# Mamba-2 block with LoRA experts in fp32: strided output-weight sums on VectorE, norm sum behind a chunk's products, gate's Silu put off

## The chip, the cores and the metric

The kernel runs on one core of a Trainium2 chip. Its time is the device time of one execution in microseconds (us); the median of several executions counts, and less is better. The core has TensorE (PE in the profile; PEld is its weight load), VectorE (DVE), ScalarE (ACT), GpSimd (POOL) and the queue SP, which issues every DMA of this kernel. Each engine, and SP, carries out its own instructions in the order in which the program holds them, and waits at an instruction whose inputs or buffers are not ready.

## The reference

For x of 2048 positions by 1024 channels, all in fp32:

```python
xn = layernorm(x)
out = x + attn(xn) + ffn(xn)

# attn: a Mamba-2 layer with 64 heads of 64 channels, 8 groups (8 heads each), state size 128
proj = xn @ in_proj_w.T                     # gate (8 x 512), x, B, C (6144), dt (64)
xBC = silu(causal_conv(hbc, kernel 4) + conv_bias)
dt = softplus(dt + dt_bias); dA = exp(-dt * exp(A_log))
state = state * dA[t] + dt[t] * x[t] * B[t]   # over time, per head
y[t] = state . C[t] + x[t] * D
yn = y * rsqrt(mean over the group's 512 channels of y*y + eps) * norm_weight * silu(gate)
attn = yn @ out_proj_w.T

# ffn: a base matrix and LoRA experts (top 2 of 8)
ffn = xn @ W_base.T + b_base + sum over the two experts of w * (xn @ A.T @ B.T) * 2
```

## The kernel before

The work is done in three stages: projections with the scan beside them, then the gates of groups 0 to 5, then the output projection. All large products use a seven-product scheme of Strassen's kind: instead of eight products of quarter matrices it takes seven of their sums, so sums of weights and of operands have to be formed beside TensorE's work.

**The stream of products.** `in_pairs` lists pairs of 128-row weight tiles of the input projection: for each of two sequence halves s and each group g, three pairs that give the raw x, B, C of the group (`raw_d`), and for groups 6 and 7 two pairs that give its gate (`gate_d`, function Silu); at the end come pairs of the base matrix. `pair` works one off in seven products of 8 TensorE instructions each, some 3.6 us a product. Its results leave through `quarter` (made by `stored`): two of four quarters are copied out of PSUM by ScalarE, two are added out of PSUM by VectorE (line 568, tile `ev` of a pool with 4 buffers), where a gate's quarter is then put through Silu by ScalarE in place (line 570). Each is stored by an SP DMA (line 572). Product 4 goes into the PSUM bank that the quarter of product 7 is read from; product 3 lies between them.

**The scan.** A block is (s, g, half): a group over 512 positions. There are 32 blocks, 16 for each s. A block has four slots, c = 0 to 3, one for each chunk of 128 positions; a slot also takes three or four products from the stream. In a slot, the loop issues in this order:

1. one product; at c = 0 `norm_mean` of the previous block (TensorE sums the squares over the channels with a matrix of ones, `ps_nv`; ScalarE takes the root, `rms`, line 866); then `scan_b` of this chunk: on TensorE the products `ps_y` (from the masked product `ms`, which lies in tile `dab`, and from `xdt`), `ps_e` (state with C) and `ps_st` (from `xdd`); on VectorE lines 813, 814 and 828 (ecp, xg, state); on GpSimd the scaling of the state (line 85)
2. `load_decays` of the chunk after next (SP); the first step of `scan_a` of the next chunk (VectorE's scan `es`, line 733)
3. one product; the second step of `scan_a`: `ps_cb` on TensorE, its copies `cbm` and `bt` (lines 744, 746) and x times D (line 751) on ScalarE, the masked product `ms` on VectorE (line 755)
4. two products or one; the third step of `scan_a`: transposes `ps_xt` on TensorE, then 8 activations `xdt` (x times dt, line 766) and 8 activations `xdd` (line 774) on ScalarE

Beside this, slots 1 and 2 hold the convolution of the next block (ScalarE line 683; VectorE line 689, 18 instructions, then Silu on ScalarE, line 677); slot 3 holds `norm_squares` (ScalarE squares, line 854; VectorE sums, lines 857 and 858); slot 0 holds `norm_gate` of the previous block (VectorE's reciprocal, line 872, and products, line 875, then the store of y). `ps_nv` and `ps_cb` share the PSUM bank `aux`.

**Sums of output weights.** In blocks 16 to 31 the loop also forms the sums of the output projection's weights, one of 16 pieces in each block (`out_sums`). A piece is a tile `wo` of 128 x 7 x 4 x 128, and a small tile `wox` of 128 x 7 x 128, one buffer each. It is loaded at the end of slot 0. GpSimd forms four contiguous sums (512 elements in a partition) in slot 1, and four strided ones over the views `t[:, :, k]` (7 runs of 128, 896 elements): two in slot 2 and two in slot 3. Stores stand between these steps. `wox` is written twice for a piece. In block 16 all of this is one slot later and the four strided sums fall into slot 3.

**Order.** The instructions are put in order by a planner, which goes by program order and by its own estimate of when inputs are ready. Some orders are fixed: `mm` and `transpose` keep TensorE in program order, as do `silu`, xdt, xdd and the squares on ScalarE. `gp` keeps GpSimd's sums and state scalings of the second half (s = 1) in program order. `pin` chains VectorE's convolution, scan, scan_b and norm_gate instructions, each behind the one pinned before it. The evictions (line 568), the masked product and the sums of squares are not pinned.

Of the kernel before, what the change touches and what calls it, by code (L numbers as in the profile page):

```python
# [9 lines left out]
AF = mybir.ActivationFunctionType  # L10
ALU = mybir.AluOpType
# [7 lines left out]
HG = H // G  # L19
# [8 lines left out]
P = 128  # L28
TS = 1024
NS = L // TS  # L30
TB = 512
Q = 128
# [11 lines left out]
def mamba_lora_kernel(  # L44
# [17 lines left out]
    nc = tc.nc  # L62
# [17 lines left out]
    def mm(*args, **kw):  # L80
        tc.keep_in_program_order(nc.tensor.matmul(*args, **kw))  # L81
# [6 lines left out]

    pinned = []

    def pin(ins):

        if pinned:
            tc.add_manual_dep(
                ins.ins, pinned[-1].ins.name,
                mybir.DependencyInfo(
                    mybir.DependencyClass.NoSync, mybir.DependencyReason.DATA
                ),
                reason="pin",
            )  # L100
        pinned.append(ins)

    def transpose(out, in_):
        tc.keep_in_program_order(nc.tensor.transpose(out, in_, ident))  # L104
# [455 lines left out]
    def stored(to, first_tile, s, func):  # L560


        def quarter(m, n, ps, add, alu=ALU.add):
            e = ev.tile([P, TB], F32, tag="ev", name="ev")
            if add is None:
                nc.scalar.activation(e, ps, func)
            else:
                nc.vector.tensor_tensor(e, ps, add, alu)
                if func != AF.Copy:
                    nc.scalar.activation(e, e, func)  # L570
            at = s * TS + n * TB
            nc.sync.dma_start(to[:, first_tile + m, at : at + TB], e)

        return quarter

    raw_d = [dram.tile([P, 6, L], F32, tag=f"raw_{g}", name=f"raw_{g}") for g in range(G)]
    gate_d = [dram.tile([P, 4, L], F32, tag=f"gate_{g}", name=f"gate_{g}") for g in range(G)]
# [51 lines left out]
    def products(n, side):  # L629

        nonlocal done
        left = list(side)
        for i in range(n):
            next(stream)
            done += 1
            take = -(-len(left) // (n - i))
            for step in left[:take]:
                step()
            left = left[take:]
        for step in left:  # L640
            step()

    def steps(gen, n):

        return [lambda: next(gen, None) for _ in range(n)]
# [54 lines left out]


    mid_of = {}
    decay_of = {}

    def load_decays(s, g, half, c):
# [18 lines left out]
    def scan_a(s, g, half, c):  # L724

        key = s, g, half, c
        n = f"{s}_{g}_{half}_{c}"
        dab, ecp = decay_of.pop(key)
        hs = slice(g * HG, (g + 1) * HG)
        cs = slice(c * Q, (c + 1) * Q)  # L730

        es = p1.tile([P, HG, Q], F32, tag="es", name=f"es_{n}")
        ins = nc.vector.tensor_tensor_scan(  # L733
            es.rearrange("p h t -> p (h t)"), dab.rearrange("p h t -> p (h t)"), here, 0.0,
            ALU.mult, ALU.add,
        )
# [18 lines left out]
        nc.vector.tensor_tensor(  # L755
            ms, es, cbm.unsqueeze(1).to_broadcast([P, HG, Q]), ALU.mult
        )
        yield
        pst = ps_one.tile([P, 4, Q], F32, tag="st", name=f"ps_xt_{n}")
        for j in range(4):  # L760
            transpose(pst[:, j, :], xg[:, j, cs])
        xdt = p2.tile([P, HG, HP], F32, tag="xdt", name=f"xdt_{n}")
        x_t = pst.rearrange("p j (a q) -> p (j a) q", q=HP)
        for h in range(HG):
            at = g * HG + h
            ins = nc.scalar.activation(  # L766
                xdt[:, h, :], x_t[:, h, :], AF.Copy,
                scale=dt_of[s][:, half * NQ + c, at : at + 1],
            )
            tc.keep_in_program_order(ins)  # L770

        xdd = p1.tile([P, HG, HP], F32, tag="xdd", name=f"xdd_{n}")
        for h in range(HG):
            ins = nc.scalar.activation(  # L774
                xdd[:, h, :], xdt[:, h, :], AF.Copy, scale=es[:, h, Q - 1 : Q]
            )
            tc.keep_in_program_order(ins)
        mid_of[key] = ms, ecp, bt, xdt, xdd, psy
        yield
# [115 lines left out]
    def add(*args):  # L895
        gp(1, *args)
# [39 lines left out]
    def out_sums(pool, i):  # L936

        p, q, kt = i // 8, i // 4 % 2, i % 4
        t = pool.tile([P, 7, 4, P], F32, tag="wo", name=f"wo_{i}")
        x = pool.tile([P, 7, P], F32, tag="wox", name=f"wox_{i}")  # L940

        def store(j, src):
            nc.sync.dma_start(w2_d[p][:, j, :, q, kt, :].rearrange("i c o -> c i o"), src)

        for j, (m, k) in enumerate(((0, 0), (0, 1), (1, 1), (1, 0))):
            nc.sync.dma_start(
                t[:, j].rearrange("c (m k) o -> c m k o", m=2),
                w_out[4 * p + 2 * k : 4 * p + 2 * k + 2, 2 * q + m, :, :, kt, :]
                .rearrange("k c m o -> c m k o"),
            )  # L950
        yield

        add(t[:, 5], t[:, 0], t[:, 3], ALU.subtract)
        add(t[:, 3], t[:, 3], t[:, 2], ALU.add)
        add(t[:, 4], t[:, 3], t[:, 0], ALU.subtract)
        add(t[:, 6], t[:, 1], t[:, 4], ALU.subtract)
        yield
        store(0, t[:, :, 0])
        store(1, t[:, :, 1])
        store(3, t[:, :, 3])  # L960
        yield
        add(x, t[:, :, 0], t[:, :, 2], ALU.subtract)
        add(t[:, :, 2], t[:, :, 2], t[:, :, 3], ALU.add)
        yield
        store(6, x)
        store(4, t[:, :, 2])
        yield
        add(x, t[:, :, 2], t[:, :, 0], ALU.subtract)
        add(t[:, :, 1], t[:, :, 1], x, ALU.subtract)
        yield  # L970
        store(5, x)
        store(2, t[:, :, 1])
        yield


# [67 lines left out]
    for _ in scan_a(*blocks[0], 0):  # L1043
        pass
# [18 lines left out]
    for b, blk in enumerate(blocks):  # L1063
        s, g, half = blk
        prev = blocks[b - 1] if b else None
        nxt = blocks[b + 1] if b + 1 < len(blocks) else None
        for c in range(NQ):
# [8 lines left out]
            n = target(slot) - done  # L1076
# [26 lines left out]
            parts = [side[i * len(side) // np_ : (i + 1) * len(side) // np_] for i in range(np_)]  # L1103
# [10 lines left out]
                    tail = steps(conv_steps, 1)  # L1114

            products(1, parts[0])
            if c == 0 and prev:
                norm_mean(*prev)
            scan_b(*blk, c)
            if 0 < q <= len(quads):  # L1120
                next(quads[q - 1])
            if b == 16 and c == 1:
                left_sums = out_sums(wo, 0)
                next(left_sums)
            elif b >= 16 and c:
                next(left_sums)
                if b == 16 and c == 3:
                    next(left_sums)
                    next(left_sums)
            if second:  # L1130
                load_decays(*second)
            next(a, None)
# [4 lines left out]
            if c == NQ - 1:  # L1137
                sq = norm_squares(*blk)
                parts[1] += steps(sq, 2)
                parts[2] += steps(sq, 1)  # L1140
            products(1, parts[1])
            next(a, None)
            products(1, parts[2])
            products(min(n - 3, 1), parts[3])
            next(a, None)
            for step in tail:
                step()
            for i in range(4, n):
# [404 lines left out]
    for t, (s, p) in enumerate(passes):  # L1553
        last = t + 1 == len(passes)
        for u, i in enumerate(units):
# [10 lines left out]
            if u < 6 or not last:  # L1566
                t1, u1 = (t, u + 1) if u < 6 else (t + 1, 0)
# [153 lines left out]
```

## Time and profile before

| | |
|---|---|
| median of 3 executions | 3442.19 us (3440.59 to 3443.03) |
| the profiled execution | 3442.68 us; its span is 3440.9 us, granted clock 0.995 |
| TensorE busy | 3359.4 us (98% of the span) |
| VectorE busy | 2471.7 us (72%) |
| ScalarE busy | 1524.9 us (44%) |
| GpSimd busy | 959.8 us (28%) |

The busy shares are means over stages that differ. Blocks 0 to 15 are worked off from 179 to 1183 us, blocks 16 to 31 from 1183 to some 2157 us, and the stages of the gates and the output follow. "Idle before" tells how long an engine stood still ahead of an instruction, and the name behind the arrow what ended that wait by the profile; where an instruction waits for more than one engine it is the one that came last. PEclk is the clock that was granted to TensorE, as a share of full speed.

### The profile page before, as it was taken

The page shows a single profiled execution, that of the slowest core. Times are in us where ns is not written, and L with a number is a line of the kernel's source. Part 1 is how long each engine was busy: PE and PEld are TensorE (multiplying, and loading weights), DVE is VectorE, ACT ScalarE, POOL GpSimd, SP SyncE. Part 2 cuts the span into 40 slices and gives each one's busy share as a digit, 9 for nine tenths or more (in the row PEclk, how much of TensorE's full clock was granted, in tenths as well). Part 3 has the DMA queues.
Part 4 walks back from the last instruction along what each step waited for, and adds up shares of the span by engine and source line. Part 5 has one row for each costly group of instructions (what it writes and reads, how often), then busy time and mean ns, then how long its engine had stood idle before and what let it go on. Part 6 is the DMA issues. An engine that isn't in the chain of part 4 may idle for free.

```text
span 3440.9 us, 41344 instructions
## 1 busy us (share of the span) xinstructions
PE 3359.4 (98%) x13828; PEld 2182.9 (63%) x13828; DVE 2471.7 (72%) x2576; ACT 1524.9 (44%) x4030; POOL 959.8 (28%) x611
## 2 busy tenths in 40 slices
PE   9999999999999999999999999999999999999999
PEld 7455555555554445445545445588888888888888
DVE  7379888889887888888888787545644566555654
ACT  2266767676665566666666655222222200000000
POOL 4122222222224333333324333465444100000000
PEclk9999999999999999999999999999999999999999
DMA  6657565666699988888888789676655686585654
GB/s 244 196 162 224 193 212 193 212 199 203 197 312 304 310 248 273 248 260 253 250 270 254 240 261 310 197 237 214 239 184 184 247 318 239 196 299 188 214 164 146
DMA packets 535572, 799.39 MB, mean 232 GB/s; under 512 B 34880, under 2 KB 264384, under 8 KB 531776
## 3 DMA queue, kind: packets, MB, share of 16 engines
q1 hardware_dynamic: 535360, 796.75, 71.4%
q8 instruction: 111, 1.82, 0.2%
q14 instruction: 101, 0.83, 0.1%
HBM read 546.00 MB, written 250.61 MB: 232 GB/s over the span
## 4 chain that ended last, share of the span: by engine, by line
PE 67%; DVE 16%; DMA 6%; ACT 4%; issue 4%; SPq 1%; POOL 1%; DVEq 0%; ACTq 0%; POOLq 0%
PE ps_x_x L81 9%; PE ps_x_w L81 8%; PE ps_y_w L81 5%; PE ps_a_w L81 5%; PE ps_a_x L81 5%; PE ps_y_x L81 5%; PE ps_x_z L81 5%; DVE xg L689 5%; PE ps_a_z L81 3%; PE ps_y_z L81 3%; DVE es L733 2%; PE ps_y L81 2%; PE ps_e L81 2%; PE ps_st L81 2%; PE ps_x_b L81 2%
## 5 line engine op out<-in xcount | busy, mean ns | idle before, releaser
L689 DVE SCALAR_TENSOR_TENSOR xg<-rawx,cw,xg 128x512 f32<-128x512 f32 x384 | 391.1, 1026 | 12.8 <-ACT xg L683 5.4
L85 POOL TENSOR_TENSOR state<-state,tot 128x512 f32<-128x512 f32 x112 | 135.1, 1206 | 812.0 <-PE ps_e L81 775.9
L733 DVE TENSOR_TENSOR_SCAN es<-dab,here 128x1024 f32<-128x1024 f32 x128 | 312.1, 2439 | 12.9 <-ACT xdd L774 7.4
L81 PE MATMUL ps_x_w<-t,w 128*128 128x256 f32 x1344 | 303.8, 379 | 0.0
L751 ACT ACTIVATE ps_y<-xg,dsk 128x128 f32<-128x128 f32 x512 | 189.8, 371 | 239.0 <-DVE xg L814 217.6
L81 PEld LDWEIGHTS ps_x_w<-t,w 128*128 128x128 f32 x1344 | 255.4, 190 | 41.5 <-issue 7.4
L774 ACT ACTIVATE xdd<-xdt,es 128x64 f32<-128x64 f32 x1024 | 262.6, 393 | 0.0
L766 ACT ACTIVATE xdt<-ps_xt,dt 128x64 f32<-128x64 f32 x1024 | 223.8, 337 | 53.7 <-PE ps_xt L104 53.7
L689 DVE SCALAR_TENSOR_TENSOR bc<-rawb,cw,bc 128x512 f32<-128x512 f32 x192 | 192.0, 1003 | 19.4 <-ACT bc L683 15.7
L81 PE MATMUL ps_a_w<-q,w 128*128 128x256 f32 x896 | 202.7, 379 | 2.8 <-DMA w<-w 2.8
L1658 ACT COPY ps_x_w<-ps_a_w 128x512 f32<-128x512 f32 x28 | 16.0, 570 | 418.7 <-PE ps_a_w L81 418.7
L813 DVE TENSOR_TENSOR ecp<-ecp,ps_e 128x512 f32<-128x512 f32 x120 | 81.8, 682 | 160.8 <-PE ps_e L81 156.5
L81 PEld LDWEIGHTS ps_a_w<-q,w 128*128 128x128 f32 x896 | 170.1, 190 | 26.6 <-issue 3.6
L81 PEld LDWEIGHTS ps_y<-dab,xdt 128*64 128x64 f32 x2048 | 112.6, 137 | 110.9 <-ACT xdd L774 81.5
L85 POOL TENSOR_TENSOR wo<-wo 128x512 f32<-128x512 f32 (+1 forms) x80 | 172.3, 2154 | 18.0 <-DMA wo<-in_w_out_dram 13.0
L81 PE MATMUL ps_a_x<-op_again,a_x 128*128 128x512 f32 x384 | 174.4, 597 | 0.0
L81 PE MATMUL ps_y_x<-op_again,s_x 128*128 128x512 f32 x384 | 174.4, 597 | 0.0
L81 PE MATMUL ps_x_x<-op_again,s_x 128*128 128x512 f32 x384 | 172.9, 593 | 1.5 <-ACT ps_x_x L511 1.5
L755 DVE TENSOR_TENSOR dab<-es,cbm 128x1024 f32<-128x1024 f32 x128 | 167.8, 1311 | 7.9 <-ACT cbm L744 7.6
L464 POOL TENSOR_TENSOR s_x<-a_x,a_x 128x512 f32<-128x512 f32 x48 | 73.6, 1534 | 355.1 <-PE ps_y_x L81 200.8
L81 PE MATMUL ps_x_x<-op,s_x 128*128 128x512 f32 x368 | 165.6, 592 | 0.0
L81 PE MATMUL ps_y_x<-op,s_x 128*128 128x512 f32 x368 | 165.5, 592 | 0.0
(320 smaller groups left out, 6884.3 us busy)
## 6 DMA issues: line engine op xcount, KB each, us to landing
w<-w SPq DMA_DIRECT2D x196, 512.0 KB, 3.6
dab<-da_d SPq DMA_DIRECT2D x128, 512.0 KB, 6.3
raw<-ev SPq DMA_DIRECT2D x192, 256.0 KB, 3.8
a_x<-in_w_in_dram SPq DMA_DIRECT2D x168, 256.0 KB, 4.4
w<-wo SPq DMA_DIRECT2D x80, 448.0 KB, 4.4
ecp<-run_d SPq DMA_DIRECT2D x256, 128.0 KB, 5.7
y<-xg SPq DMA_DIRECT2D x64, 512.0 KB, 3.4
rawx<-raw SPq DMA_DIRECT2D x24, 1030.0 KB, 7.3
```

Source lines behind the costliest of these rows:

```text
L81: tc.keep_in_program_order(nc.tensor.matmul(*args, **kw))
L85: ins = nc.gpsimd.tensor_tensor(*args)
L464: nc.gpsimd.tensor_tensor(t[what], t[x], t[y], alu)
L689: ins = nc.vector.scalar_tensor_tensor(dst[:, i, :], raw[:, i, k : k + TB], cw[:, ti, k : k + 1], dst[:, i, :], ALU.mult, ALU.add,)
L733: ins = nc.vector.tensor_tensor_scan(es.rearrange("p h t -> p (h t)"), dab.rearrange("p h t -> p (h t)"), here, 0.0, ALU.mult, ALU.add,)
L751: nc.scalar.activation(psy[:, j, :], xg[:, j, cs], AF.Copy, scale=dsk[:, at : at + 1])
L755: nc.vector.tensor_tensor(ms, es, cbm.unsqueeze(1).to_broadcast([P, HG, Q]), ALU.mult)
L766: ins = nc.scalar.activation(xdt[:, h, :], x_t[:, h, :], AF.Copy, scale=dt_of[s][:, half * NQ + c, at : at + 1],)
L774: ins = nc.scalar.activation(xdd[:, h, :], xdt[:, h, :], AF.Copy, scale=es[:, h, Q - 1 : Q])
L813: pin(nc.vector.tensor_tensor(ecp, ecp, pse, ALU.mult))
L1658: nc.scalar.copy(px, pa)
```

## The change

Three things are moved; the computation stays the same.

- The four strided sums of an output-weight piece go from GpSimd to VectorE, all in slot 3 of the block, in the steps behind the third product. The first is put behind the latest masked product (`behind`), and all four enter the chain of `pin`. The sum that was written into `wox` a second time is now written over `t[:, :, 0]`. The four stores that need them follow at the end of slot 3; the contiguous sums stay on GpSimd in slot 1 (block 16: slot 2), their stores at the end of that slot.
- `norm_mean` is issued behind `scan_b` of slot 0 instead of ahead of it.
- For the two quarters of a gate that VectorE evicts, the Silu and the store are put off: they are kept in a list and issued by `do_put_off`, behind the third step of `scan_a` (xdt and xdd), and behind each product that follows in the slot.

```diff
+    def behind(ins, other):
+        tc.add_manual_dep(ins.ins, other.ins.name, ..., reason="pin")
...
             else:
                 nc.vector.tensor_tensor(e, ps, add, alu)
-                if func != AF.Copy:
+            at = s * TS + n * TB
+
+            def rest():
+                if add is not None and func != AF.Copy:
                     nc.scalar.activation(e, e, func)
-            at = s * TS + n * TB
-            nc.sync.dma_start(to[:, first_tile + m, at : at + TB], e)
+                nc.sync.dma_start(to[:, first_tile + m, at : at + TB], e)
+
+            if add is None or func == AF.Copy:
+                rest()
+            else:
+                put_off.append(rest)
...
+    def do_put_off():
+        while put_off:
+            put_off.pop(0)()
...
-        nc.vector.tensor_tensor(
-            ms, es, cbm.unsqueeze(1).to_broadcast([P, HG, Q]), ALU.mult
-        )
+        masked[:] = [
+            nc.vector.tensor_tensor(
+                ms, es, cbm.unsqueeze(1).to_broadcast([P, HG, Q]), ALU.mult
+            )
+        ]
...
-        add(x, t[:, :, 0], t[:, :, 2], ALU.subtract)
-        add(t[:, :, 2], t[:, :, 2], t[:, :, 3], ALU.add)
+        t0, t1, t2, t3 = (t[:, :, k] for k in range(4))
+        ins = nc.vector.tensor_tensor(x, t0, t2, ALU.subtract)
+        behind(ins, masked[0])
+        pin(ins)
+        pin(nc.vector.tensor_tensor(t2, t2, t3, ALU.add))
+        pin(nc.vector.tensor_tensor(t0, t2, t0, ALU.subtract))
+        pin(nc.vector.tensor_tensor(t1, t1, t0, ALU.subtract))
         yield
         store(6, x)
-        store(4, t[:, :, 2])
-        yield
-        add(x, t[:, :, 2], t[:, :, 0], ALU.subtract)
-        add(t[:, :, 1], t[:, :, 1], x, ALU.subtract)
-        yield
-        store(5, x)
-        store(2, t[:, :, 1])
+        store(4, t2)
+        store(5, t0)
+        store(2, t1)
         yield
...
             products(1, parts[0])
+            scan_b(*blk, c)
             if c == 0 and prev:
                 norm_mean(*prev)
-            scan_b(*blk, c)
...
+            sums_at = (2, 3) if b == 16 else (1, 3)
+            if b >= 16 and c == sums_at[0] or b == 16 and c == 1:
                 next(left_sums)
...
                 parts[1] += steps(sq, 2)
                 parts[2] += steps(sq, 1)
+                if b >= 16:
+                    parts[2] += [lambda: next(left_sums)]
...
             next(a, None)
+            do_put_off()
             for step in tail:
                 step()
             for i in range(4, n):
                 products(1, parts[i])
+                do_put_off()
...
-            if b > 16 or b == 16 and c > 1:
-                if c == 0:
-                    left_sums = out_sums(wo, b - 16)
+            if b > 16 and c == 0:
+                left_sums = out_sums(wo, b - 16)
+                next(left_sums)
+            if b >= 16 and c in sums_at:
                 next(left_sums)
```

More of the change, by code (lines that the diff above doesn't have):

```diff
@@ L89, in mamba_lora_kernel @@
     pinned = []
+    def behind(ins, other):
+        tc.add_manual_dep(
+            ins.ins, other.ins.name,
+            mybir.DependencyInfo(mybir.DependencyClass.NoSync, mybir.DependencyReason.DATA),
+            reason="pin",
+        )
     def pin(ins):
         if pinned:
[L94 to L99, printed above, removed]
-            )
+            behind(ins, pinned[-1])
         pinned.append(ins)
@@ L568, in quarter @@
                 nc.vector.tensor_tensor(e, ps, add, alu)
-                if func != AF.Copy:
+            at = s * TS + n * TB
+            def rest():
+                if add is not None and func != AF.Copy:
                     nc.scalar.activation(e, e, func)
-            at = s * TS + n * TB
-            nc.sync.dma_start(to[:, first_tile + m, at : at + TB], e)
-        return quarter
+                nc.sync.dma_start(to[:, first_tile + m, at : at + TB], e)
[3 more added lines that the diff above has]
+                put_off.append(rest)
+        return quarter
+    put_off = []
+    def do_put_off():
+        while put_off:
+            put_off.pop(0)()
     raw_d = [dram.tile([P, 6, L], F32, tag=f"raw_{g}", name=f"raw_{g}") for g in range(G)]
@@ L702, in mamba_lora_kernel @@
     mid_of = {}
+    masked = []
     decay_of = {}
@@ L754, in scan_a @@
         ms = dab
-        nc.vector.tensor_tensor(
-            ms, es, cbm.unsqueeze(1).to_broadcast([P, HG, Q]), ALU.mult
-        )
+        masked[:] = [
+            nc.vector.tensor_tensor(
+                ms, es, cbm.unsqueeze(1).to_broadcast([P, HG, Q]), ALU.mult
+            )
+        ]
         yield
@@ L1123, in mamba_lora_kernel @@
                 left_sums = out_sums(wo, 0)
+            sums_at = (2, 3) if b == 16 else (1, 3)
+            if b >= 16 and c == sums_at[0] or b == 16 and c == 1:
                 next(left_sums)
[L1125 to L1129, printed above, removed]
             if second:
```

## The prediction

> **What bounds the kernel now.** I read the page first, then the busy time by stage, then who TensorE waits for in the stage that the change works on, then the timeline around the longest of these waits.
>
> ```profile
> PE 3359.4 (98%) x13828; PEld 2182.9 (63%) x13828; DVE 2471.7 (72%) x2576; ACT 1524.9 (44%) x4030; POOL 959.8 (28%) x611
> ```
>
> TensorE has work for 3359.4 of 3440.9 us, so only its 81.5 us of idle time, and time at a lower clock, can be won. By stage (start and end, length, then PE busy, PEld, DVE, ACT, POOL, granted clock, DMA):
>
> ```profile
> 179.00:1183.00 1004.00, 980.33 (x3873) 514.09 (x3872) 858.57 (x1008) 660.22 (x1858) 278.69 (x186) 0.99 0.69 225
> 1183.00:2157.00 974.00, 938.80 (x3697) 485.19 (x3697) 815.74 (x756) 602.80 (x1750) 359.25 (x188) 0.99 0.86 261
> ...
> 1248.00:1253.00 5.00, 4.88 (x27) 3.38 (x28) 0.06 (x1) 1.67 (x2) 0.02 (x1) 0.66 0.41 131
> 1907.00:1915.00 8.00, 6.11 (x10) 2.86 (x11) 3.87 (x5) 7.71 (x22) 0.00 (x0) 0.57 1.04 344
> ```
>
> 1183 to 2157 us is blocks 16 to 31, where the output weights are summed: TensorE idles 974.0 - 938.8 = 35.2 us there. The last two rows show a second cost: behind a long stall the clock is granted at 0.66 over 5 us (5 x 0.34 = 1.7 us lost) or 0.57 over 8 us (3.4 lost). Stretches at 1224, 1777 and 2115 us also read 0.66, so the clock costs 4 x 1.7 + 3.4 = 10.2 us more. The stage can give 45 us at most. Who ends TensorE's waits in it (total, times, longest):
>
> ```profile
> PE ps_xt L104 <- ACT xg L677: 7.5, 4, 3.5
> PE ps_y L81 <- ACT xdt L766: 6.7, 2, 4.4
> PE ps_nv L81 <- DVE sq L858: 3.7, 1, 3.7
> PE ps_nv L81 <- ACT xdt L766: 3.3, 3, 1.1
> ...
> PE ps_nv L81 <- ACT xdd L774: 2.5, 2, 1.7
> PE ps_y L81 <- issue: 2.5, 1, 2.5
> ```
>
> Behind these, on the other engines:
>
> ```profile
> POOL wox L85 <- DMA w<-wox: 55.1, 9, 16.6
> ...
> ACT ev L570 <- DVE ev L568: 20.2, 5, 6.6
> ```
>
> The timeline shows how they become stalls:
>
> ```profile
> 1770.78 3.09 DVE L755 TENSOR_TENSOR dab<-es,cbm 128x1024 f32<-128x1024 f32 x1
> ...
> 1775.96 0.63 ACT L570 ACTIVATE ev<-ev 128x512 f32<-128x512 f32 x1 [6.58 <-DVE ev L568]
> ...
> 1776.85 2.13 PE L81 MATMUL ps_y<-dab,xdt 128*64 128x128 f32 x16 [4.37 <-ACT xdt L766]
> ...
> 2102.19 2.08 POOL L85 TENSOR_TENSOR wox<-wo 128x896 f32<-128x896 f32 x1 [16.63 <-DMA w<-wox]
> ```
>
> At 1775.96 ScalarE stood 6.58 us at a gate's Silu, waiting for the eviction on VectorE; x times dt was queued behind it and TensorE stalled 4.37 us. VectorE was late because GpSimd's strided sums ran: the masked product took 3.09 us (1.22 alone, at 1547.27). At 2102.19 the second strided sum waited for the store of wox's earlier contents; the state's scaling stood behind it in GpSimd's queue, VectorE waited 5.59 us for that at 2107.46, and TensorE 2.48 at 2114.77.
>
> **The sums.** The change takes 64 instructions (4 in each of 16 blocks) off GpSimd and puts them on VectorE.
>
> ```profile
> L689 DVE SCALAR_TENSOR_TENSOR xg<-rawx,cw,xg 128x512 f32<-128x512 f32 x180 | 192.4, 1075 | 4.1 <-ACT xg L683 0.2
> L85 POOL TENSOR_TENSOR wox<-wo 128x896 f32<-128x896 f32 x32 | 75.3, 2354 | 56.5 <-DMA w<-wox 55.1 <-DMA ecp<-run_d 1.4
> ...
> L1464 DVE TENSOR_TENSOR t<-q 128x1024 f32<-128x1024 f32 x28 | 34.1, 1219 | 3.6 <-DMA q<-yg 3.6
> ```
>
> Price on VectorE: 512 elements from SBUF take 686 ns (acc from acc and e, in the last stage, where GpSimd is idle), 1024 take 1219, so 896 take 686 + 533 x 384/512 = 1086 ns; 64 are 69.5 us, 4.34 a block. No row shows VectorE on the strided view; bounds are 0.69 us (no row of 512 is shorter) and 2.7 us (GpSimd's 75.3 + 55.2 + 42.0 us for its 64). I take 1.09: on GpSimd the stride costs nothing (2.07 us for 896 at best, 1.27 for 512, both about 2.4 ns an element). What goes: a conv step (L689) takes 0.75 us alone and 1075 ns (xg, 180) or 1165 ns (bc, 90) on average here, an excess of 58.5 + 37.4 = 96 us; the scan, the masked product and the rest add about 35. The strided sums are 172.5 of the 289.7 us of GpSimd's weight sums, so some 60% of 131 us, 78 us, leaves VectorE. Its total thus hardly changes; the load moves from the third slot, which it fills, to the end of the fourth, behind the masked product and, by program order, behind the norm's squares. There is room:
>
> ```profile
> 1548.40 0.68 DVE L858 TENSOR_TENSOR sq<-sq 128x512 f32<-128x512 f32 x1
> 1552.48 0.69 DVE L813 TENSOR_TENSOR ecp<-ecp,ps_e 128x512 f32<-128x512 f32 x1 [3.40 <-PE ps_e L81]
> ...
> 1549.24 1.10 PE L81 MATMUL ps_nv<-sq,ones 128*128 128x512 f32 x2 [1.11 <-ACT xdt L766]
> ```
>
> VectorE idles 3.40 us there (2.3 to 5.7 in the other blocks). The sums overrun it by about 1 us, and L813, L814, L828 and the next scan wait behind them. The cover for that is the next masked product: it ended at 1561.08 and was first needed at 1564.31, 3.2 us later. So 0, and with the cover gone 1 us a block. The four stores now stand together in SP's queue behind the last sum, ahead of later loads; those have about a slot in hand, 0 again. An eviction caught behind the sums can cost 4.34 + 0.68 - 3.6 (one product of cover) = 1.4 us; as two evictions in 34 us of products meet a 4.3 us stretch only in a few blocks, 4 us in all.
>
> Stalls that this ends: 2.48 us at 2114.77 with 1.7 of clock; 3.74 at 1248.12 with 1.7 (strided sums had stretched conv, squares and mask in block 16); 3.47 at 1908.89 with 3.4 (ps_xt behind a late conv, in part a Silu). Together 16.5 us. Smaller waits behind conv (the rest of ps_xt on xg, ps_x_x and ps_x_g on ev, ps_x_x on a ScalarE copy, ps_y and ps_st on xdd) are 10 us; I count half, 5. Not ended: 2.76 us and its 1.7 at 1224.55, where the sums left on GpSimd run.
>
> **The Silu.** ScalarE's work is the same; its place is behind the 16 activations of xdt and xdd, and its store moves with it past SP's later entries; the gate is read blocks later. The tile ev is held some 5 us longer, of 4 buffers at 4 evictions in some 25 us or more: 0. Gain: 4.37 us at 1776.85 with 1.7, and 2.30 at 1946.68: 8.4 us. What is late next is the conv chain itself.
>
> **The norm's sum.** ps_nv starts 0.16 us behind the end of L858 (1549.08), so its real releaser is that sum, though the view names xdt. The chunk's products need the masked product, which ended 0.6 us sooner. Over the blocks with such a wait this gives 0.6 us each in 21, 24, 29 and 30, 1.2 in 19 and 1.2 in the whole first stage: 4.8 us. It moves 3.0 us later (ps_y, ps_e, ps_st), which also covers L858. Against it: xdd, which the wait had covered, is now met by ps_st, 0.2 us in a dozen blocks, 3 us at most.
>
> **Sum.** 16.5 + 5 + 8.4 + 4.8 = 34.7 us, less 4 + 3 = 7: a gain of 27.7. The profiled execution took 3442.7 us, 1.8 beyond its span and 0.5 above the median of 3442.2; that gives 3415.
>
> The Trainium skill (TensorE: Matmul & The Clock Gate, Why this matters for your kernels) warns only of idle gaps above about 3 us; here the clock fell behind 2.48 and 2.76 us too. By that rule 2115's 1.7 us would not count and the sum would be 3416; the trace disagrees. The Trainium skill (SBUF — State Buffer, Who interferes with whom) lets a VectorE instruction with two SBUF inputs and a reading GpSimd instruction block each other, whichever came second. It speaks against the new sums where they meet the state's scaling. By that rule, at 1.04 us (the scaling's row at 2106.38) in 15 blocks, VectorE would lose up to 16 us, most of it inside the 3.2 us cover; the long conv rows agree with it.
>
> **Rivals.** *Sums at GpSimd's price.* At 2.07 us each a block's sums are 8.3 us; less 3.4 idle and 3.2 cover, 1.7 us stall TensorE in each of 15 block ends, 26 us, and half of them lose 1.7 of clock, 13: 39 against 27.7 of gain, 3453. It decides above about 1.9 us a sum. Against it: the straight line through VectorE's own rows. *The norm's bank.* ps_cb reuses ps_nv's bank aux and comes one product (3.4 us) behind it; the root took from 0.3 to 5.4 us to start after ps_nv, mostly 1.2 to 2.8, and lasts 0.69. Were it late by 1.5 us in all 31 blocks, 46 us would be lost: 3461. *Half of it.* The slots stay late, since conv still runs beside the contiguous sums, and the fourth slot only swaps contention for sums: 8.4 + 4.2 + 4.8 - 7 = 10 us, 3432. *No difference.* Instructions fall into another order and as many stalls form elsewhere: 3442.
>
> **Numbers.** Forecast 0.62, half of it 0.17, no difference 0.07, sums dear 0.09, bank 0.05. About 0.2% (7 us) is what a measurement can tell. The first two give faster 0.79; the last two slower 0.14. The range starts at 3400, the stage's 45 us nearly all won, and ends at 3441, which takes in the half gain and no difference and leaves out the slower cases.
>
> **What would show it.** Right: strided rows on VectorE near 1.09 us; L689 in blocks 16 to 31 below 950 ns; no GpSimd wait for wox; no wait of L570 ahead of xdt; TensorE's idle time in the second stage near 17 us instead of 35, and one 0.66 stretch left in it. Wrong: L813 waiting behind sums and ps_y for the masked product in the second slot, ps_cb waiting for the root, or ps_x_x for evictions behind sums.

## The result, and the profile after

The changed kernel takes **3408.34 us** (median of 4, 3407.0 to 3414.4) against 3442.61 us beside it: a ratio of **0.9905 [0.9888, 0.9922]**, 34.3 us less. The forecast was 3415, a gain of 27.7. The page's line of busy times:

```profile
PE 3351.6 (98%) x13828; PEld 2181.4 (64%) x13828; DVE 2474.4 (73%) x2640; ACT 1522.1 (45%) x4030; POOL 779.9 (23%) x547
```

VectorE has 64 instructions more and yet only 2.7 us more busy time; GpSimd loses 179.9 us. By stage (blocks 0 to 15, then 16 to 31, then five microseconds out of the second; columns as before: start and end, length, busy time of PE, PEld, DVE, ACT, POOL, granted clock, DMA share, GB/s):

```profile
178.00:1187.00 1009.00, 982.79 (x3871) 516.18 (x3870) 856.86 (x1007) 657.00 (x1854) 273.75 (x186) 0.99 0.69 224
1187.00:2123.00 936.00, 927.07 (x3698) 480.08 (x3697) 819.50 (x823) 603.57 (x1755) 185.79 (x124) 1.00 0.91 272
1229.00:1234.00 5.00, 4.78 (x11) 2.24 (x12) 4.96 (x6) 4.66 (x19) 0.00 (x0) 0.66 0.70 227
```

The second stage is 38 us shorter (974.0 to 936.0), the first 5 us longer (1004 to 1009), and TensorE idles 8.9 us in the second where it idled 35.2. The last row is the one stretch at a lower clock left in it, in block 16, where the forecast left one. Who ends TensorE's waits in this stage now (total, times, longest):

```profile
PE ps_y L81 <- ACT xdd L792: 3.4, 2, 2.5
PE ps_xt L105 <- DVE state L846: 2.0, 1, 2.0
PE ps_x_b L81 <- DVE ev L569: 1.7, 1, 1.7
```

Of the three costly lines of before, ps_xt behind conv and ps_nv behind the squares are gone, and ps_y behind xdt is down from 6.7 us to 0.4. The groups of the same stage, one shape a line (busy time, mean ns of one, idle time before):

```profile
L704 DVE SCALAR_TENSOR_TENSOR xg<-rawx,cw,xg 128x512 f32<-128x512 f32 x180 | 149.1, 834 | 5.8 <-ACT xg L698 1.8
L704 DVE SCALAR_TENSOR_TENSOR bc<-rawb,cw,bc 128x512 f32<-128x512 f32 x90 | 103.8, 1161 | 3.6 <-ACT bc L698 2.0
L831 DVE TENSOR_TENSOR ecp<-ecp,ps_e 128x512 f32<-128x512 f32 x64 | 43.6, 682 | 54.5 <-PE ps_e L81 50.0 <-DMA w<-wo 3.2 <-DMA s_x<-s_x_d 1.3
L986 DVE TENSOR_TENSOR wo<-wo 128x896 f32<-128x896 f32 x16 | 20.4, 1272 | 0.5
L985 DVE TENSOR_TENSOR wo<-wo 128x896 f32<-128x896 f32 x16 | 19.0, 1188 | 0.4
L984 DVE TENSOR_TENSOR wo<-wo 128x896 f32<-128x896 f32 x16 | 17.4, 1090 | 0.5
L981 DVE TENSOR_TENSOR wox<-wo 128x896 f32<-128x896 f32 x16 | 17.3, 1084 | 0.0
```

The last four lines are the strided sums, 74.1 us together. Each finds its predecessor just ended (idle 0.0 to 0.5 us over 16). The conv steps of xg (L704, L689 before) fell from 1075 to 834 ns; those of bc, beside the contiguous sums that stay on GpSimd, stayed at 1161. Two lines of the kernel before, in the same stage, go with this: bc's steps, and VectorE's wait for ps_e ahead of ecp.

```profile
L689 DVE SCALAR_TENSOR_TENSOR bc<-rawb,cw,bc 128x512 f32<-128x512 f32 x90 | 104.6, 1165 | 4.4 <-ACT bc L683 2.6
```

```profile
DVE ecp L813 <- PE ps_e L81: 102.3, 34, 6.6
```

The means hide two kinds of steps. Before, 115 of the 180 steps of xg ran beside no GpSimd instruction and took 748 ns on average (753 at most); the 30 that overlapped a strided sum alone took 2235 ns. In the changed kernel 148 run alone, at 747 ns.

VectorE's wait for ps_e ahead of ecp (L831) is 50.0 us here and was 102.3 us: the sums took the idle time that the prediction pointed to, 52 us in 16 blocks, 3.3 us each.

A second profile of the same kernel (below) has TensorE idle for 25.0 us in the first stage and 12.4 in the second, with the stages 1003.2 and 929.4 us long where the first profile has 1009.0 and 923.8 (blocks 0 to 15, and block 16 to the beginning of the last slot). The split between the stages thus moves by some 6 us from one execution to the next while the total moves by 0.6; a single profile tells no more of a stage than that.

### The profile page after: what moved, and what is told of

It is laid out like the page before. It is cut to its first block, busy times and chain, and to the rows that moved or that the text cites. A ratio compares the mean times of both kernels' runs of the same rounds, so it can differ in the third digit from the quotient of the medians.

```text
span 3407.6 us, 41304 instructions
## 1 busy us (share of the span) xinstructions
PE 3351.6 (98%) x13828; PEld 2181.4 (64%) x13828; DVE 2474.4 (73%) x2640; ACT 1522.1 (45%) x4030; POOL 779.9 (23%) x547
## 4 chain that ended last, share of the span: by engine, by line
PE 77%; DVE 12%; ACT 4%; DMA 3%; issue 3%; SPq 0%; POOL 0%; DVEq 0%; ACTq 0%; POOLq 0%
PE ps_x_x L81 11%; PE ps_x_w L81 9%; PE ps_a_x L81 7%; PE ps_y_x L81 7%; PE ps_a_w L81 6%; PE ps_y_w L81 6%; PE ps_x_z L81 5%; DVE xg L704 3%; PE ps_y_z L81 3%; PE ps_a_z L81 3%; PE ps_e L81 3%; PE ps_y L81 3%; PE ps_st L81 2%; PE ps_x_b L81 2%; DVE es L749 2%
## 5 line engine op out<-in xcount | busy, mean ns | idle before, releaser
L704 DVE SCALAR_TENSOR_TENSOR xg<-rawx,cw,xg 128x512 f32<-128x512 f32 x384 | 342.2, 899 | 16.8 <-ACT xg L698 5.9
L749 DVE TENSOR_TENSOR_SCAN es<-dab,here 128x1024 f32<-128x1024 f32 x128 | 297.8, 2326 | 14.5 <-DMA dab<-da_d 10.2
L704 DVE SCALAR_TENSOR_TENSOR bc<-rawb,cw,bc 128x512 f32<-128x512 f32 x192 | 191.0, 1001 | 18.4 <-ACT bc L698 15.0
L772 DVE TENSOR_TENSOR dab<-es,cbm 128x1024 f32<-128x1024 f32 x128 | 164.8, 1287 | 10.3 <-ACT cbm L760 10.0
L81 PE MATMUL ps_a_x<-op,a_x 128*128 128x512 f32 x368 | 165.5, 592 | 0.0
L831 DVE TENSOR_TENSOR ecp<-ecp,ps_e 128x512 f32<-128x512 f32 x120 | 81.8, 682 | 103.9 <-PE ps_e L81 97.8
```

The costliest lines, as they stand in the source:

```text
L704: ins = nc.vector.scalar_tensor_tensor(dst[:, i, :], raw[:, i, k : k + TB], cw[:, ti, k : k + 1], dst[:, i, :], ALU.mult, ALU.add,)
L749: ins = nc.vector.tensor_tensor_scan(es.rearrange("p h t -> p (h t)"), dab.rearrange("p h t -> p (h t)"), here, 0.0, ALU.mult, ALU.add,)
L772: nc.vector.tensor_tensor(ms, es, cbm.unsqueeze(1).to_broadcast([P, HG, Q]), ALU.mult)
L831: pin(nc.vector.tensor_tensor(ecp, ecp, pse, ALU.mult))
```

## The experiments

Each was compared with the kernel before on the same chip. TensorE's idle time in the second stage is taken from the first to the last block, from one profile each.

| kernel | median, us | ratio to before | idle in stage 2, us |
|---|---|---|---|
| before | 3443.5, 3442.8, 3442.8 | | 35.2 |
| changed, once more | 3409.1 | 0.9905 [0.9889, 0.9921] | 12.4 |
| sums alone | 3409.9 | 0.9902 [0.9888, 0.9915] | 13.9 |
| norm's sum alone | 3441.7 | 0.9994 [0.9985, 1.0003] | 34.4 |
| Silu alone | 3434.7 | 0.9973 [0.9961, 0.9984] | 31.8 |
| sums and Silu | 3408.5 | 0.9897 [0.9884, 0.9911] | 12.6 |
| strided sums on GpSimd, issued in slot 3 | 3446.1 | 1.0010 [1.0001, 1.0019] | 35.6 |
| sums on VectorE in the old slots | 3404.7 | 0.9883 [0.9868, 0.9898] | 7.9 |
| first sum five times | 3442.9 | 1.0000 [0.9991, 1.0009] | 35.6 |
| contiguous sums on VectorE too | 3428.0 | 0.9956 [0.9943, 0.9968] | 24.1 |
| the same, contiguous sums later | 3413.9 | 0.9920 [0.9905, 0.9934] | 12.0 |
| old slots, norm late only in stage 2 | 3405.6 | 0.9893 [0.9876, 0.9909] | 12.5 |
| strided sums left out | 3415.2 | 0.9921 [0.9906, 0.9936] | 14.9 |

### The parts, one at a time

The change came in three parts, so the first four kernels are the kernel before with one or two of them. The sums alone, shown against the changed kernel, leave out the other two:

```diff
+            if c == 0 and prev:
+                norm_mean(*prev)
             scan_b(*blk, c)
-            if c == 0 and prev:
-                norm_mean(*prev)
...
-            if add is None or func == AF.Copy:
-                rest()
-            else:
-                put_off.append(rest)
+            rest()
```

> The strided sums go to VectorE in slot 3 as in the change; norm_mean stays ahead of scan_b and a gate's Silu and store stay where they were. Theory A (the strided sums on GpSimd caused most of the second stage's stalls, by slowing VectorE and by holding up GpSimd's queue): 3415 to 3421 us; TensorE's idle time in blocks 16 to 31 falls from 35 to 15 to 20 us, and the first stage keeps its 1004 us. Rival B (the sums only have room because the norm's sum moved): ps_nv waits more than 10 us in blocks 16 to 31 behind the squares' sums, and the time stays above 3430.

Measured: 3409.9 us, 33.6 less than before. Nearly all of the gain, and more than the forecast gave this part. Its waits of TensorE in the second stage:

```profile
PE ps_nv L81 <- DVE sq L873: 4.3, 1, 4.3
PE ps_y L81 <- ACT xdt L781: 3.5, 3, 2.3
PE ps_xt L105 <- DVE state L843: 2.8, 1, 2.8
```

The stall of 4.37 us behind a gate's Silu is down to 1.01 us here, with the Silu where it was: VectorE's eviction comes sooner, and ScalarE stands 3.21 us at that Silu (1753.57) where it stood 6.58. The other one put down to the Silu, 2.30 us in block 28, is still there with 2.31; in the changed kernel's two profiles it is 0.89 and 2.33, where the masked product comes last (it ends 0.1 us before ps_y starts).

The norm's sum alone, in the kernel before:

```diff
+            scan_b(*blk, c)
             if c == 0 and prev:
                 norm_mean(*prev)
-            scan_b(*blk, c)
```

> The kernel before with norm_mean behind scan_b and nothing else. Theory A (it saves some 3 us in the second stage and costs some 5 in the first, where the root stands behind x times D on ScalarE and ps_cb waits for it): 3441 to 3446 us, first stage 1007 to 1010 us. Rival B (it gives what the prediction counted, 4.8 us less up to 3): 3438 to 3441, first stage 1003 to 1005.

Measured: 3441.7 us, ratio 0.9994 [0.9985, 1.0003]: nothing that can be told from no change.

The Silu alone, in the kernel before:

```diff
-                if func != AF.Copy:
+            at = s * TS + n * TB
+
+            def rest():
+                if add is not None and func != AF.Copy:
                     nc.scalar.activation(e, e, func)
...
+            if add is None or func == AF.Copy:
+                rest()
+            else:
+                put_off.append(rest)
...
+            do_put_off()
```

> The kernel before with a gate's Silu and store put off and nothing else. Theory A (the Silu held x times dt up): 3433 to 3437 us; the stalls of 4.37 us at 1777 and 2.30 us at 1947 shrink below 1 us each. Rival B (these stalls came from VectorE being late, so that something else waits in the Silu's place): within 2 us of 3442.

Measured: 3434.7 us, 8.7 less: the size that the prediction gave it, but not by its parts. The stall of 2.30 us in block 28 goes, and the one of 4.37 falls only to 1.79, where VectorE's masked product, 3.1 us long beside a strided sum, now comes last. Waits of some 0.5 us in blocks 17 and 23 grow to 2.26 and 2.21. TensorE's idle time in the stage falls by 3.4 us (35.2 to 31.8), the time at half clock by 6.8.

Sums and Silu together, against the changed kernel:

```diff
+            if c == 0 and prev:
+                norm_mean(*prev)
             scan_b(*blk, c)
-            if c == 0 and prev:
-                norm_mean(*prev)
```

> The changed kernel with norm_mean back ahead of scan_b. Theory A (moving the norm's sum costs 5 us in the first stage and gives at most 4 in the second): 3403 to 3409 us, first stage 1003 to 1005 us, no wait of ps_cb for rms. Rival B (the norm's place is needed as cover for the sums): 3413 us or more, ps_nv waiting in most of blocks 17 to 31.

Measured: 3408.5 us. On top of the sums the Silu gives 1.4 us, which the intervals do not tell from nothing, and the norm's sum on top of both nothing (3408.3 to 3409.1). The three parts alone add up to 33.6 + 8.7 + 1.7 = 44.0 us, together they give 34: some 10 us are reached by two parts each.

### Engine or place

The sums change engine, slot and the number of times that wox is written. The next kernel puts them back on GpSimd, issued in the new slot and in place, without `behind`:

```diff
-        ins = nc.vector.tensor_tensor(x, t0, t2, ALU.subtract)
-        behind(ins, masked[0])
-        pin(ins)
-        pin(nc.vector.tensor_tensor(t2, t2, t3, ALU.add))
-        pin(nc.vector.tensor_tensor(t0, t2, t0, ALU.subtract))
-        pin(nc.vector.tensor_tensor(t1, t1, t0, ALU.subtract))
+        add(x, t0, t2, ALU.subtract)
+        add(t2, t2, t3, ALU.add)
+        add(t0, t2, t0, ALU.subtract)
+        add(t1, t1, t0, ALU.subtract)
```

> The changed kernel with its four strided sums put back on GpSimd, still in the fourth slot and still in place, so that wox is written once a block and nothing waits for its store. It tells engine from place. If the gain comes from the engine (strided sums off the conv steps' and VectorE's shared access), GpSimd's 8 to 9 us of sums now stretch the fourth slot's scan, masked product and evictions, and the state's scaling, queued behind them on GpSimd, is late in the next slot: TensorE waits for the state or for xdd, and the time is 3425 to 3450. If what counts is only that the sums leave the third slot, and that the wait for wox's store is gone, the conv steps of xg stay short and the time is that of the changed kernel, 3406 to 3413.

Measured: 3446.1 us, 1.0010 [1.0001, 1.0019]: the whole gain is gone, although no sum waits for wox's store. Its groups and its longest wait of TensorE, in the second stage:

```profile
L704 DVE SCALAR_TENSOR_TENSOR xg<-rawx,cw,xg 128x512 f32<-128x512 f32 x180 | 180.0, 1006 | 5.8 <-ACT xg L698 1.8
L85 POOL TENSOR_TENSOR wo<-wo 128x896 f32<-128x896 f32 x45 | 132.5, 2944 | 3.5
```

```profile
PE ps_y L81 <- ACT xg L692: 14.1, 5, 3.4
```

An in-place strided sum on GpSimd takes 2944 ns here against 1084 to 1272 on VectorE, and VectorE's conv steps are at 1006 ns again. The sums did not all stay in the fourth slot. Nothing holds them there: they start some 3.3 us into a slot, behind the state's scaling in GpSimd's queue. In the odd blocks, whose fourth slot has no scaling (the state is not needed any more), they start in the third slot, beside the conv steps, and TensorE waits at the beginning of slot 3: the five waits of the second fence are in blocks 17, 19, 23, 27 and 29. The view names xg, but the masked product ended 0.1 us before each. In the eight even blocks the sums do start in the fourth slot, and there the masked product is late beside them: five times it takes 3.09 us or a little more and ends 0.1 to 0.3 us before a late ps_y in the next block, 9.8 us of stalls in all. So issuing the sums later, and in place, is worth nothing on GpSimd. GpSimd sums held back behind the masked product, as VectorE's are, were not tried.

The counterpart keeps VectorE and goes back to the old slots, two sums in slot 2 and two in slot 3, without `behind`:

```diff
-        ins = nc.vector.tensor_tensor(x, t0, t2, ALU.subtract)
-        behind(ins, masked[0])
-        pin(ins)
+        pin(nc.vector.tensor_tensor(x, t0, t2, ALU.subtract))
         pin(nc.vector.tensor_tensor(t2, t2, t3, ALU.add))
+        yield
+        store(6, x)
+        store(4, t2)
+        yield
         pin(nc.vector.tensor_tensor(t0, t2, t0, ALU.subtract))
         pin(nc.vector.tensor_tensor(t1, t1, t0, ALU.subtract))
...
```

> The changed kernel with its four strided sums on VectorE, but in the slots of the kernel before: two in the third slot, two in the fourth. If the engine is what counts, nearly all of the gain stays: conv steps of xg near 0.8 us, time 3406 to 3415. If the place counts (the third slot is full on VectorE: 15.1 us busy of 17.5 before, and it gets 2.2 us of sums while its 12 conv steps lose some 2.9 us of stretch), half or less of the gain stays and TensorE waits for conv again (ps_xt for xg): 3420 to 3435.

Measured: 3404.7 us (3401.4 to 3405.8), all of the gain and perhaps 4 us more; the intervals of the two ratios overlap. The engine is the cause: in the old slots it is worth 38 us, and writing in place, which this kernel does too, gave nothing on GpSimd. The sums here take 1085 to 1092 ns each, with none of the stretch that the last two show in the changed kernel.

### How much cover lies under the sums

The forecast priced the sums on VectorE at nothing, by 3.4 us of idle time and 3.2 us of cover behind it, 6.6 us a block. To see the edge, the first sum was repeated, which doubles a block's sums:

```diff
+        for _ in range(4):
+            pin(nc.vector.tensor_tensor(x, t0, t2, ALU.subtract))
```

> The changed kernel with the first strided sum done five times instead of once (the same result each time), which makes a block's sums 8 instructions and about 8.7 us in place of 4.6: the cover under the sums tried from the far side. By the prediction's threshold (3.4 us of idle time and 3.2 us of cover) a block's end loses about 2.1 us in each of 15 blocks, 31 us, and clock behind half of them, 13 us: 3435 to 3452, with ps_y waiting for the masked product in the second slot. If more cover lies behind (the next slots' own idle time and several products in hand), the loss is under 1 us a block: 3409 to 3423.

Measured: 3442.9 us, the prediction's side. In the second stage:

```profile
L985 DVE TENSOR_TENSOR wox<-wo 128x896 f32<-128x896 f32 x60 | 73.5, 1224 | 1.9
L831 DVE TENSOR_TENSOR ecp<-ecp,ps_e 128x512 f32<-128x512 f32 x61 | 41.5, 681 | 13.2 <-PE ps_e L81 13.2
```

```profile
PE ps_y L81 <- issue: 18.1, 8, 2.5
PE ps_xt L105 <- DVE state L846: 5.0, 5, 2.0
```

The idle time ahead of ecp is used up (13.2 us of once 102.3), and eight times TensorE stands at ps_y at the beginning of slot 1, up to 2.5 us: the masked product of the second slot is late, the very sign that the prediction named. The view says "issue", but the masked product ended 0.1 us before each of the eight, and xdt, which ps_y also reads, 3.4 us before or more. By the five groups of sums (73.5 here, 68.3 in the other four) a block's sums are 141.8/15 = 9.45 us. TensorE's idle time grew by 23 to 27 us, 1.5 to 1.8 a block, so by idle time the cover is some 7.8 us a block on average: a little more than the 6.6 counted.

The opposite leaves the four instructions out and keeps their stores:

```diff
-        ins = nc.vector.tensor_tensor(x, t0, t2, ALU.subtract)
...
-        pin(nc.vector.tensor_tensor(t1, t1, t0, ALU.subtract))
         yield
-        store(6, x)
+        store(6, t0)
```

> The changed kernel with its four strided sums left out (the output weights' sums are then not what the reference needs; loads, stores and the contiguous sums stay): what the sums still cost on VectorE. If the cover holds, as the prediction has it, nothing of it is on the path: 3403 to 3409. If the sums still cost TensorE time at the block ends (2 us in half the blocks or more), 3385 to 3398.

Measured: 3415.2 us, some 6 us longer than with the sums on the same chip, though the intervals of the two ratios overlap; neither theory said so. The waits of VectorE and of ScalarE in the second stage, two views:

```profile
DVE ecp L831 <- PE ps_e L81: 112.1, 39, 7.9
```

```profile
ACT bc L698 <- DMA rawb<-raw: 31.8, 11, 6.2
```

VectorE's 74 us went into waiting (112.1 us ahead of ecp, 50.0 with the sums), so no cost of the sums to TensorE shows. In exchange ScalarE now stands 31.8 us at the first activation of the next bc, whose rows have not landed; the wait of 5.88 us at 2004.63 has the Silu of xg queued behind it, and TensorE idles 1.76 us behind that at 2008.33. That an emptier VectorE brings these activations forward in ScalarE's queue fits, but was not tried by itself.

### The contiguous sums too

bc's conv steps are still stretched by the four contiguous sums. They were moved as well:

```diff
-        add(t[:, 5], t[:, 0], t[:, 3], ALU.subtract)
-        add(t[:, 3], t[:, 3], t[:, 2], ALU.add)
-        add(t[:, 4], t[:, 3], t[:, 0], ALU.subtract)
-        add(t[:, 6], t[:, 1], t[:, 4], ALU.subtract)
+        ins = nc.vector.tensor_tensor(t[:, 5], t[:, 0], t[:, 3], ALU.subtract)
+        behind(ins, masked[0])
+        pin(ins)
+        pin(nc.vector.tensor_tensor(t[:, 3], t[:, 3], t[:, 2], ALU.add))
+        pin(nc.vector.tensor_tensor(t[:, 4], t[:, 3], t[:, 0], ALU.subtract))
+        pin(nc.vector.tensor_tensor(t[:, 6], t[:, 1], t[:, 4], ALU.subtract))
```

> The changed kernel with the four contiguous sums of a block moved from GpSimd to VectorE too, behind the masked product of their slot; GpSimd keeps only the state's scaling in blocks 16 to 31. If sharing between GpSimd and VectorE is the cost, the conv steps of bc fall from 1161 to about 760 ns (6 a block, 2.4 us), which pays for most of the added 4 x 0.68 = 2.7 us, and the stalls at 1229 and in blocks 30 and 31 go: 3403 to 3408. If the second slot is full, the added work makes conv later and TensorE waits for xg or for evictions: 3412 to 3425.

Measured: 3428.0 us, 19 worse than the changed kernel and beyond both expectations, although bc's steps fell as hoped. The groups of the second stage, and behind them TensorE's longest wait:

```profile
L704 DVE SCALAR_TENSOR_TENSOR bc<-rawb,cw,bc 128x512 f32<-128x512 f32 x90 | 70.8, 801 | 4.2 <-ACT bc L698 2.8
L971 DVE TENSOR_TENSOR wo<-wo 128x512 f32<-128x512 f32 x16 | 11.0, 689 | 28.7 <-DMA wo<-in_w_out_dram 20.4 <-issue 4.5 <-DMA a_x<-in_w_in_dram 3.9
```

```profile
PE ps_y L81 <- ACT xdd L792: 15.1, 8, 4.0
```

VectorE stands 28.7 us in nine blocks ahead of the first contiguous sum, 20.4 of it put down to the loads of the output weights. GpSimd stood at the same loads in the changed kernel (26.4 us of its waits) with little behind it: VectorE waited 5.8 us in all for the state's scaling. Behind VectorE's own wait stand the next scan and masked product, and TensorE waits for those (second fence: the view names xdd, which ps_y does not read; the masked product, which it reads, ended 0.1 to 0.3 us before each of these). To separate this from VectorE's load, the same sums were issued at the end of their slot:

```diff
-            if b >= 16 and c == sums_at[0] or b == 16 and c == 1:
+            if b == 16 and c == 1:
                 next(left_sums)
...
             for step in tail:
                 step()
+            if b >= 16 and c == sums_at[0]:
+                next(left_sums)
```

> The kernel with all weight sums on VectorE, but its four contiguous sums issued at the very end of their slot, behind the conv steps and the next chunk's scan and masked product, so that the loads of the output weights have some 4 to 8 us more to land. If the loss of the all-VectorE kernel (19.6 us against the changed kernel) was VectorE standing at the loads (28.7 us in nine blocks), the wait for the loads falls under 5 us, conv of bc stays near 0.8 us, and the time is 3400 to 3409. If it was VectorE's load itself (2.8 us more a block in a full third slot), the waits for the loads go but TensorE waits for xdt or the state: 3420 to 3432.

Measured: 3413.9 us: 14 of the 19 us come back, between the two expectations. VectorE has no wait for these loads left, and bc's steps are at their shortest:

```profile
L704 DVE SCALAR_TENSOR_TENSOR bc<-rawb,cw,bc 128x512 f32<-128x512 f32 x90 | 67.0, 753 | 3.6 <-ACT bc L698 2.0
L971 DVE TENSOR_TENSOR wo<-wo 128x512 f32<-128x512 f32 x16 | 11.8, 737 | 0.0
```

Yet against the changed kernel nothing is won (12.0 us of idle time in stage 2 against 12.4): the 37 us taken off bc's steps are paid for with 49 us of contiguous sums on VectorE. Whether bc's stretch ever cost TensorE anything was not tried.

### Norm's sum by stage

The last two are run side by side on one chip: the changed kernel again, and the two-and-two kernel with

```diff
+            if c == 0 and prev and s == 0:
+                norm_mean(*prev)
             scan_b(*blk, c)
-            if c == 0 and prev:
+            if c == 0 and prev and s:
                 norm_mean(*prev)
```

> The changed kernel itself, once more, beside the next three on one chip, so that differences of a few us between variants are read there: 3406 to 3411 from every theory.

> The changed kernel with two changes that the runs so far point to: the strided sums on VectorE two in the third and two in the fourth slot, and the norm's sum ahead of the chunk's products in blocks 0 to 15 and behind them only in blocks 16 to 31. If the norm's sum behind the products is what makes blocks 0 to 15 longer (idle 23.7 us before, 25 to 27 in every run with the move), these blocks need 1003 to 1005 us, the waits ps_cb for the root and ps_st for xdd go there, and the time is 3399 to 3404. If blocks 0 to 15 differ for other reasons (instruction order in general), nothing is gained: 3403 to 3408.

Measured: 3409.1 us (3404.0 to 3414.9) and 3405.6 us (3404.3 to 3407.3). Blocks 0 to 15 take 1003.2 and 1003.0 us, with 25.0 and 25.7 us of TensorE idle: nothing gained. The waits of ps_cb for the root and of ps_st for xdd mostly go (2.6 and 4.9 us in the changed kernel; 1.0 us of the second is left), and ps_nv waiting for the squares (2.7), 2.4 us more of ps_xt behind the state (3.8 in place of 1.4) and 2.3 us more at the evictions of x (8.0 in place of 5.7) come back. Splitting the sums two and two was 3.5 to 4.4 us faster in both kernels that did it, with overlapping intervals each time; it is the likely better version, not a shown one.

## Why the prediction was right, point by point

- **The main step holds:** VectorE was late because GpSimd's strided sums ran beside it. With the engine put back the gain goes; with the slots put back it stays; and the slow conv steps are those that overlap a GpSimd sum (2235 ns against 748).
- **The total is nearer than its parts, by luck:** against the forecast's gain of 27.7 us stand 34.3, but the sums were given 16 us too little, the Silu beside them 7.0 too much (8.4 against 1.4), and the norm's sum 1.8 where nothing came.
- **The price of a strided sum** was 1086 ns; the first two take 1084 and 1090. The other two, 1188 and 1272 on average, meet the state's scaling on GpSimd, and who started first decides. Six sums that started beside a running scaling took 1.81 to 1.94 us and ended 0.95 us behind it; the sums that started first took 1.08 to 1.09 us, and the scaling ended 0.9 to 1.0 us behind them. The Trainium skill (SBUF — State Buffer, Who interferes with whom) says that a VectorE instruction with two SBUF inputs and a GpSimd instruction that reads SBUF block each other, whichever comes second; the trace agrees. By 16 x (101 + 185) ns it cost 4.6 us of VectorE's time, where the prediction allowed up to 16.
- **VectorE's total "hardly changes"**: 2471.7 to 2474.4 us. With 74.1 us of sums added, the relief was 71 us where 78 was estimated.
- **The cover** was sized at 6.6 us a block and measured at some 7.8; at 4.6 us of sums it costs nothing. The rival of dear sums was a real threshold, but further off: at 9.45 us a block, 2.36 a sum, the time is only back at before's, where the prediction set the turn at 1.9.
- **The term that was too small: stalls ended by the sums.** The forecast gave them 16.5 + 5 - 4 = 17.5 us, and 33.6 came. Of the small waits behind conv half was counted, 5 us, and ps_nv's were booked under the norm's sum; all ten waits of 0.69 to 1.89 us in blocks 17 to 30, 12.15 us together, are gone with the sums alone or down to 0.3 us (two of them). Of the 4.37 us and its clock that were booked under the Silu, 3.4 us also end by the sums. Added up: 3.74 + 3.47 + 2.48 + 12.15 + 3.36 = 25.2 us of idle time ended, less a new stall of 4.3, is 20.9; the trace has 35.2 - 13.9 = 21.3. The time that the records show at half clock fell from 20.5 to 10.2 us, worth 5.1. That explains 26.4 of the 29.0 us by which this stage is shorter in the profiles.
- **The terms counted twice: Silu and norm.** 8.4 us meets the Silu alone in size (8.7), not in its parts, and is wrong beside the sums (1.4). The norm's sum was given 4.8 against a loss of 3; alone its 1.7 is inside what can't be told from no change. Its five short waits in blocks 19 to 30 are among the ten that the sums end by themselves. The 1.2 us given for the first stage did not come.
- **The feared bank** showed itself: ps_cb waited for the root in the first stage, 3.26 us at 1062.59 in the first profile and 2.6 us in all in the second. Its size was one or two blocks, not 31.
- **"The four stores ... 0"** missed a cost at another store. In block 30 two contiguous stores, where one stood before, now go ahead of the next decays' load in SP's queue; that load lands 10.3 and 12.6 us after its issue in the two profiles, 8.5 before. The scan waits 5.6 and 7.9 us for it, and TensorE stalls 2.5 and 4.8 us in block 31. With the sums two and two, one store stands there again, the load lands after 9.1 us, that scan waits 0.6 us and the stall is down to 0.7. The next scan then waits 5.1 us for its own load, which stands behind two stores of sums as it did before, where VectorE came later and had no such wait. So the place of the stores and an emptier VectorE, which comes sooner, both seem to have a part; the stores were not moved by themselves.
- **The signs:** conv of xg below 950 ns (834), no wait of a sum for wox, none of a gate's Silu ahead of xdt, idle time near 17 (8.9 and 12.4 us). One stretch at a lower clock was left in the first profile; in the second, 13.7 us at half clock, so that sign does not hold from run to run. A stall's length alone does not tell whether the clock falls: in the profiles of before and of the changed kernel it fell to one half for 3.4 us behind single stalls of 1.95 and 2.00 us, and did not fall behind others of 2.30 and 2.52.

## What to carry to other kernels

An engine with idle time can still be the wrong one: what GpSimd's sums cost was paid by VectorE, whose instructions took up to three times as long beside them (2235 ns against 748). Before stalls are added up by the part of a change that ends them, ask which other part ends the same stall, since three parts worth 44 us alone gave 34 together. And an instruction that must wait for a load belongs on an engine with nothing urgent queued behind it.

## What the runs showed of the hardware

A sum over a strided view of 896 elements in a partition costs VectorE no more per element than a contiguous one (1084 ns; 689 ns for 512 contiguous, so 1.2 to 1.35 ns an element in both). On GpSimd the same sum took 2.07 us at best, and three of a block's four took 2.94 on average when issued in the fourth slot, with VectorE busy beside them: GpSimd's instructions are stretched as well as VectorE's, and its state scalings too (1090 ns without strided sums, 1259 with them on VectorE in the fourth slot, where they meet, and 1332 with the first sum repeated). Leaving out 74 us of work on an engine off the critical path made the kernel no faster and rather some 6 us slower, so differences of that size between such variants need not have one cause that can be named.
